# Layer 0 of a four-layer kernel: where VectorE takes the channel statistics, and which PSUM bank the gate's first product uses

## The chip, the core and the metric

The kernel runs on one core of a Trainium2 chip, in float32 throughout. The metric is the device time of one execution in microseconds (us), lower is better. TensorE is written PE (its weight loads PEld), VectorE DVE, ScalarE ACT, GpSimd POOL, and SyncE, which issues most of the DMAs, SP.

## What is computed

Four layers in a row on a batch of four 64 x 64 images with 128 channels. The change lies in layer 0, and in what layer 0 hands to layer 1. Cut to those, the reference is:

```python
# layer 0: neighbourhood attention (7 x 7 keys for each pixel, 4 heads of 32), gated
qkv = (x @ qkv_w + qkv_b).reshape(B, H, W, 3, HEADS, HEAD_DIM)
scores = einsum('bxyhd,bxyklhd->bxyhkl', q, kwin) + bias
attn_out = einsum('bxyhkl,bxyklhd->bxyhd', softmax(scores), vwin) @ proj_w + proj_b
gate = sigmoid(relu(x @ g1_w + g1_b) @ g2_w + g2_b)
x = attn_out * gate + x

# layer 1: begins with a group norm over the whole image, 32 groups of 4 channels
mean, var = mean and variance of x over (H, W, the 4 channels of a group)
h = (x - mean) * rsqrt(var + 1e-6) * scale + bias
# then full attention over the 4096 pixels, and x + o
```

The statistics of the title are the mean and the variance of each channel of layer 0's output, which layer 1's group norm needs. The gate's first product is `x @ g1_w`. Layers 2 and 3 (a gated product with a layer norm, and a selective scan in four directions) are not touched.

## The kernel before

**Stages.** The four images go through layer 0 and layer 1 one after the other. Layers 2 and the front part of 3 of an image run inside layer 1's loop and shortly after it; the scans of layer 3 and the output come at the end, for all four. Layer 0 of the next image begins (its first two chunks and its first score blocks) beside the last steps of the image before; a generator is advanced by two steps at a time there (lines 1107 and 1108).

**Layer 0's loop.** An image of 4096 pixels is 32 blocks of 8 x 16 pixels, and 8 chunks of 512 pixels; a chunk is four blocks. The loop at line 522 runs over `i`, and in one turn works on several blocks at different ages. In this order:

- `score(i + 3)`: four products q k, one for each head (32 rows of the contraction each, L456), into four PSUM banks; then four reductions on DVE (L460) that add the bias and take the maximum;
- `value(i - 1)`: the product with v (L502) into a bank `po`, which ACT copies to `oT` (L507);
- `normalise(i + 1)`: a reciprocal on DVE (L480), four scalings on POOL (L482);
- `project(i - 2)`: the product with proj (L512) into a bank `pp`, which DVE adds to x with the gate (L513);
- `by_key(i, 0)` and `by_key(i, 1)`: transposes of the probabilities (L491), copied out by ACT and by DVE (L493);
- `soften(i + 2)`, first half: two exponentials on ACT (L474);
- `take_in(n + 2, part)`, one of four parts of a chunk that is two chunks ahead: part 0 transposes x (and makes `gate_of` of the chunk before, L402), part 1 the products `pq` and `pk`, part 2 the product `pv` (L384), which DVE empties into `vt` (L386), part 3 the gate's first product `pg` (L391), which ACT empties with a Relu (L393);
- `by_key(i, 2)`, with ACT's copy, and the second half of `soften(i + 2)`;
- every fourth turn from `i` = 6 on, `hand_on(n)`: the four finished blocks of chunk n are transposed (L412), ACT copies them to `hT` (L414), and DVE takes the statistics of that copy (`bn_stats`, L415).

So in four turns of the loop there is one of each part of `take_in` and one `hand_on`. Part 2 falls in the turn just after a `hand_on`, part 3 in the turn after that. The gate's product and `pv` come up to chunk 7, that is in turns up to `i` = 20 and 19; there are eight `hand_on`, at `i` = 6, 10, ... 34.

**What sets the order.** Each engine works its instructions off in its own order. In layer 0 the instructions of PE, ACT and DVE are pinned (`pin`, L349): they stay in the order in which the program writes them. An instruction that waits holds all those behind it on its engine.

**PSUM.** There are eight banks, in three rings: "s" (four banks, `ps_s`, L149), "t" (two, `ps_t`, L152) and "o" (two, `ps_o`, L155). A new tile of a ring takes the bank of the tile that was taken one full ring earlier, and its first product waits until that tile has been emptied. The scores take four "s" banks in each turn; `pq`, `pk`, `pv` and `pg` take one each. After `pv`, the fourth score of the next turn takes the bank of `pv`; after `pg`, the fourth score of the next turn takes the bank of `pg`. In "o" lie `po`, `pp` and the gate's second product `pg2` (L400).

Of the kernel before, what the change touches and what calls it, by code (L numbers as in the profile page):

```python
# [34 lines left out]
CH = 512  # L35
NCH = L // CH
HEADS, HD, KS = 4, 32, 7
NEG = -1.0e30
GH = 64
# [99 lines left out]
def layers_0_to_2(  # L139
    ctx, tc, xf, mata, matb, rows, rpb, convw, sel, ident, cl, dram, big, ring, early, x3_d, ub_d, zf_d, y_d, dbl_d, ct_d, gw_d, bw_d  # L140
):
    nc = tc.nc
    wp = ctx.enter_context(tc.tile_pool(name="wa", bufs=1))
    tmp = ctx.enter_context(tc.tile_pool(name="tmp", bufs=2))
    sml = ctx.enter_context(tc.tile_pool(name="sml", bufs=3))
    psp = ctx.enter_context(tc.tile_pool(name="psA", bufs=1, space=PSUM))


    def ps_s(shape, name):  # L149
        return psp.tile(shape, F32, name=name, tag="s", bufs=4)  # L150

    def ps_t(shape, name):  # L152
        return psp.tile(shape, F32, name=name, tag="t", bufs=2)

    def ps_o(shape, name):  # L155
        return psp.tile(shape, F32, name=name, tag="o", bufs=2)
# [11 lines left out]
    def m(name, p=P):  # L168
        a, e = MA[name]
        return ma[0:p, a:e] if e <= nma else once[0:p, a - nma:e - nma]  # L170

    def rw(name, tiles=None):
        a, e = ROW[name]
        r = row[:, a:e] if e <= nrow else once[:, NMA - nma + a - nrow:NMA - nma + e - nrow]
        return r if tiles is None else r.unsqueeze(1).to_broadcast([P, tiles, r.shape[-1]])
# [25 lines left out]
    for cv, n in enumerate(cols_of):  # L201
        t = t_d[cv].rearrange("q h d k -> (q h) (d k)")
# [85 lines left out]
    def in_blocks(t, n=4):  # L288

        return t.rearrange("p (r b c) -> p r b c", b=n, c=BC)  # L290
# [46 lines left out]
    def layer_0(b, xt, edge_t):  # L337
# [5 lines left out]
        hT = ring([P, L], f"hT_{b}")  # L343
        st = sml.tile([P, NCH, 6], F32, name="st1", tag="st1", bufs=1)
# [4 lines left out]
        def pin(ins):  # L349
            return tc.keep_in_program_order(ins)  # L350
# [3 lines left out]
        def take_in(n, part):  # L354


            if part == 0 and n > 0:
                gate_of(n - 1)
            if n == NCH:
                return  # L360
            if part == 0:
                pt = ps_t([P, 4, P], "pt")
                for k in range(4):
                    pin(nc.tensor.transpose(pt[:, k, :], xt[:, 4 * n + k, :], ident))
                x = part_of[n] = tmp.tile([P, CH], F32, name="xT", tag="xT", bufs=4)
                pin(nc.scalar.copy(in_blocks(x), pt.rearrange("p b (r c) -> p r b c", c=BC)))
            elif part == 1:
                x = part_of[n]
                pq = ps_s([P, CH], "pq")
                pin(nc.tensor.matmul(pq, lhsT=ma[:, q0:q0 + C], rhs=x, start=True, stop=True))  # L370
                pin(nc.scalar.activation(
                    qT[:, 4 * n:4 * n + 4, :].rearrange("p b (r c) -> p r b c", c=BC), in_blocks(pq), AF.Identity,
                    bias=sbq0, scale=HD ** -0.5,
                ))
                pk = ps_s([P, CH], "pk")
                pin(nc.tensor.matmul(pk, lhsT=ma[:, k0:k0 + C], rhs=x, start=True, stop=True))
                pin(nc.scalar.activation(
                    kT[:, BR * n:BR * n + BR, :].rearrange("p r w -> p (r w)"), pk, AF.Identity, bias=cl("bk0")
                ))
            elif part == 2:  # L380
                x = part_of[n]
                pv = ps_s([P, 4, C], "pv")
                for k in range(4):
                    pin(nc.tensor.matmul(pv[:, k, :], lhsT=x[:, bass.ts(k, P)], rhs=ma[:, v0:v0 + C], start=True, stop=True))  # L384
                vt = tmp.tile([P, 4, C], F32, name="vt", tag="c512", bufs=9)
                pin(nc.vector.tensor_tensor(vt, pv, rw("bv0", 4), ALU.add))  # L386
                nc.sync.dma_start(v_d[b][CH * n:CH * n + CH, :].rearrange("(k p) c -> p k c", p=P), vt)
            else:
                x = part_of.pop(n)
                pg = ps_s([GH, CH], "pg")  # L390
                pin(nc.tensor.matmul(pg, lhsT=m("g1"), rhs=x, start=True, stop=True))  # L391
                g1 = tmp.tile([GH, 4, P], F32, name="g1", tag="g1")
                pin(nc.scalar.activation(  # L393
                    g1.rearrange("p b (r c) -> p r b c", c=BC), in_blocks(pg), AF.Relu, bias=cl("g1b", p=GH)
                ))
                part_of[n] = g1

        def gate_of(n):
            g1 = part_of.pop(n)
            pg2 = ps_o([P, 4], "pg2")  # L400
            for k in range(4):
                pin(nc.tensor.matmul(pg2[:, k:k + 1], lhsT=g1[:, k, :], rhs=cl("g2w", p=GH), start=True, stop=True))  # L402
            g = gate[:, 4 * n:4 * n + 4]
            pin(nc.scalar.activation(g, pg2, AF.Exp, bias=ng2b, scale=-1.0))
            pin(nc.vector.tensor_scalar(g, g, 1.0, None, ALU.add))
            pin(nc.vector.reciprocal(g, g))

        def hand_on(n):

            pt = ps_t([P, 4, P], "pt")  # L410
            for k in range(4):
                pin(nc.tensor.transpose(pt[:, k, :], xt[:, 4 * n + k, :], ident))  # L412
            h = hT[:, bass.ts(n, CH)]
            pin(nc.scalar.copy(h, pt.rearrange("p k t -> p (k t)")))  # L414
            pin(nc.vector.bn_stats(st[:, n, :], h))  # L415

        def bias_in(i):

# [50 lines left out]
        def soften(i, heads):  # L469
            k = blocks[i]  # L470
            if heads[0] == 0:
                k.sm = sml.tile([P, HEADS], F32, name="sm0", tag="sm0", bufs=4)
            for h in heads:
                pin(nc.scalar.activation(  # L474
                    k.pr[:, h], k.pr[:, h], AF.Exp, bias=k.mx[:, h:h + 1], accum_out=k.sm[:, h:h + 1]
                ))

        def normalise(i):
            k = blocks[i]
            pin(nc.vector.reciprocal(k.sm, k.sm))  # L480
            for h in range(HEADS):
                nc.gpsimd.tensor_scalar(k.pr[:, h], k.pr[:, h], k.sm[:, h:h + 1], 1.0, ALU.mult, ALU.mult)  # L482
            k.prT = []

        def by_key(i, g, evac):
            k = blocks[i]
            if g < len(k.tiles):
                at, n, _ = k.tiles[g]
                pt = ps_t([P, HEADS, P], "pt0")
                for h in range(HEADS):  # L490
                    pin(nc.tensor.transpose(pt[0:n, h, :], k.pr[:, h, at:at + n], ident))  # L491
                prT = tmp.tile([P, HEADS, P], F32, name="prT0", tag="c512", bufs=9)
                pin(evac(prT[0:n], pt[0:n]))  # L493
                k.prT.append(prT)

        def value(i):
            k = blocks[i]
            po = ps_o([P, P], "po0")
            for g, (at, n, slot) in enumerate(k.tiles):
                for h in range(HEADS):  # L500
                    hp = slice(HD * h, HD * h + HD)
                    pin(nc.tensor.matmul(  # L502
                        po[hp, :], lhsT=vs[0:n, slot, hp], rhs=k.prT[g][0:n, h, :],
                        start=(g == 0), stop=(g == len(k.tiles) - 1),
                    ))
            k.oT = tmp.tile([P, P], F32, name="oT0", tag="oT")
            pin(nc.scalar.copy(k.oT, po))  # L507

        def project(i):
            k = blocks.pop(i)  # L510
            pp = ps_o([P, C], "pp0")
            pin(nc.tensor.matmul(pp, lhsT=k.oT, rhs=m("proj"), start=True, stop=True))  # L512
            pin(nc.vector.scalar_tensor_tensor(xt[:, i, :], pp, gate[:, i:i + 1], xt[:, i, :], ALU.mult, ALU.add))  # L513
# [8 lines left out]
        for i in range(-3, NT + 5):  # L522
            if i + 3 < NT:
                score(i + 3)
            if 0 <= i - 1 < NT:
                value(i - 1)
            if 0 <= i + 1 < NT:
                normalise(i + 1)
            if 0 <= i - 2 < NT:
                project(i - 2)  # L530
            if 0 <= i < NT:
                by_key(i, 0, nc.scalar.copy)
                by_key(i, 1, nc.vector.tensor_copy)
            if 0 <= i + 2 < NT:
                soften(i + 2, (0, 1))
            n, part = divmod(i + 3, 4)
            if n + 2 < NCH or (n + 2, part) == (NCH, 0):
                take_in(n + 2, part)
            if 0 <= i < NT:
                by_key(i, 2, nc.scalar.copy)  # L540
            if 0 <= i + 2 < NT:
                soften(i + 2, (2, 3))
            if i >= 6 and (i - 6) % 4 == 0 and (i - 6) // 4 < NCH:
                hand_on((i - 6) // 4)
        handed[b] = hT, st


# [935 lines left out]
```

## Time and profile before

| | us |
|---|---|
| three runs, median (lowest to highest) | 3831.19 (3826.19 to 3833.25) |
| the profiled execution, its time | 3828.72 |
| its span, first to last instruction | 3826.9 |
| the four stretches of layer 0, from the first score to the last statistics | 33 to 217, 799 to 961, 1579 to 1741, 2354 to 2515 |
| busy in the second of these, 162.00 us: PE, PEld, DVE, ACT, POOL | 152.32, 104.01, 98.02, 126.65, 82.82 |

The stretches are taken from the timeline: the first score matmul of an image, and the sum-up of its statistics at layer 1's begin (L550). The first stretch holds waits for DMAs at the kernel's start as well. A profile shows one execution; its times are those of that execution, and a busy PE is not PE at its peak, since matmuls overlap. In the rows of a timeline the columns are: start, length, engine, line, operation, what is written and read, shape, number of instructions merged in the row, and in brackets how long the engine stood idle before it and what ended that. A row "x8" of L456 holds the four heads' scores, two passes for each head.

### The profile page before, as it was taken

The page shows a single profiled execution, that of the slowest core. Times are in us where ns is not written, and L with a number is a line of the kernel's source. Part 1 is how long each engine was busy: PE and PEld are TensorE (multiplying, and loading weights), DVE is VectorE, ACT ScalarE, POOL GpSimd, SP SyncE. Part 2 cuts the span into 40 slices and gives each one's busy share as a digit, 9 for nine tenths or more (in the row PEclk, how much of TensorE's full clock was granted, in tenths as well). Part 3 has the DMA queues.
Part 4 walks back from the last instruction along what each step waited for, and adds up shares of the span by engine and source line. Part 5 has one row for each costly group of instructions (what it writes and reads, how often), then busy time and mean ns, then how long its engine had stood idle before and what let it go on. Part 6 is the DMA issues. An engine that isn't in the chain of part 4 may idle for free.

```text
span 3826.9 us, 69375 instructions
## 1 busy us (share of the span) xinstructions
PE 3401.1 (89%) x26780; PEld 2787.6 (73%) x26780; DVE 2829.9 (74%) x4865; ACT 2681.4 (70%) x4350; POOL 1420.2 (37%) x1562
## 2 busy tenths in 40 slices
PE   6999999999899999998999999989999987666647
PEld 4679989966799889667998897669888863222236
DVE  3657777756677788666787886667877866999968
ACT  3865667778676776686766776866767756999934
POOL 5510012245122122352122223522221326999866
PEclk8999999999999999999999999999999996555579
DMA  5100000131010012310211112100101148999998
GB/s 141 47 3 25 12 18 29 43 99 35 18 42 32 32 62 82 121 43 1 74 66 48 51 52 94 46 1 23 41 31 59 57 166 220 232 220 204 213 276 280
DMA packets 205199, 319.30 MB, mean 83 GB/s; under 512 B 23583, under 2 KB 112188, under 8 KB 200732
## 3 DMA queue, kind: packets, MB, share of 16 engines
q1 hardware_dynamic: 165572, 237.57, 18.2%
q0 software_dynamic: 19776, 68.56, 9.8%
q10 hardware_dynamic: 19520, 8.73, 0.8%
q8 instruction: 211, 3.46, 0.4%
q14 instruction: 120, 0.98, 0.1%
HBM read 150.91 MB, written 155.56 MB: 80 GB/s over the span
## 4 chain that ended last, share of the span: by engine, by line
PE 49%; DVE 24%; ACT 9%; POOL 8%; issue 6%; DMA 2%; SPq 1%; POOLq 0%; ACTq 0%; DVEq 0%
PE po L640 15%; PE sc L607 14%; POOL inp L1210 4%; DVE mx L619 4%; DVE acc L858 3%; DVE st L633 3%; POOL y L1249 3%; PE pt L491 3%; DVE mx L614 3%; PE sc L456 2%; PE po L502 2%; ACT st L634 2%; ACT pr L474 2%; ACT st L610 2%; PE pz L808 1%
## 5 line engine op out<-in xcount | busy, mean ns | idle before, releaser
L640 PE MATMUL po<-v,st 128*128 128x129 f32 x8192 | 1081.3, 275 | 4.1 <-ACT st L634 4.1
L607 PE MATMUL sc<-qT,kT 128*128 128x128 f32 x8192 | 1081.9, 276 | 0.4 <-ACT st L610 0.4
L607 PEld LDWEIGHTS sc<-qT,kT 128*128 128x128 f32 x8192 | 1003.5, 193 | 21.9 <-issue 18.1
L640 PEld LDWEIGHTS po<-v,st 128*128 128x128 f32 x8192 | 998.8, 192 | 5.4 <-issue 5.4
L610 ACT COPY st<-sc 128x512 f32<-128x512 f32 x1024 | 577.8, 583 | 527.0 <-PE sc L607 519.6
L633 DVE TENSOR_TENSOR st<-st,pb 128x2048 f32<-128x2048 f32 x256 | 573.9, 2283 | 47.7 <-PE pb L630 47.1
L614 DVE TENSOR_TENSOR mx<-mx,st 128x1024 f32<-128x1024 f32 x256 | 315.3, 1232 | 239.3 <-ACT st L610 237.4
L634 ACT ACTIVATE st<-st 128x2048 f32<-128x2048 f32 x256 | 483.4, 1908 | 6.4 <-DVE st L633 4.7
L1199 PE MATMUL pdt<-dbl,dt 8*128 8x512 f32 x512 | 309.0, 1082 | 142.4 <-ACT de L1206 142.0
L1210 POOL TENSOR_TENSOR inp<-de,ub 128x1024 f32<-128x1024 f32 x128 | 412.1, 4479 | 36.0 <-ACT de L1206 29.0
L1199 PEld LDWEIGHTS pdt<-dbl,dt 8*128 8x128 f32 x512 | 114.4, 312 | 334.1 <-ACT de L1206 270.7
L704 POOL TENSOR_TENSOR x<-x,row 128x512 f32<-128x512 f32 x32 | 49.9, 1559 | 788.9 <-PE pt L274 788.9
L482 POOL TENSOR_SCALAR pr<-pr,sm 128x308 f32<-128x308 f32 (+3 forms) x512 | 243.5, 494 | 259.8 <-DVE sm L480 187.6
L849 POOL TENSOR_TENSOR gsum<-gsum,tp 128x504 f32<-128x504 f32 (+1 forms) x176 | 254.1, 1446 | 122.7 <-ACT gsum L837 83.9
L474 ACT ACTIVATE pr<-pr,mx 128x308 f32<-128x308 f32 (+3 forms) x512 | 262.5, 517 | 0.0
L619 DVE TENSOR_TENSOR mx<-mx 128x512 f32<-128x512 f32 (+2 forms) x384 | 256.9, 669 | 6.1
L1234 DVE TENSOR_TENSOR_SCAN h<-h,end,inp 128x1024 f32<-128x1024 f32 x96 | 221.1, 2346 | 14.7 <-POOL inp L1210 7.0
L491 PE MATMUL pt<-ident,pr 128*88 128x128 f32 (+5 forms) x1472 | 204.1, 276 | 7.8 <-ACT prT L493 7.8
L1249 POOL DMA_DIRECT2D y<-yo x112 | 206.5, 2823 | 7.3 <-DVE yo L1248 3.8
L460 DVE CUSTOM_DVE_ANT_0 pr<-sc,bias_m 128x266 f32<-128x266 f32 (+1 forms) x384 | 151.7, 451 | 69.6 <-PE sc L456 64.7
L858 DVE SCALAR_TENSOR_TENSOR acc<-xh,cc,acc 128x512 f32<-128x512 f32 (+3 forms) x244 | 196.4, 832 | 3.8 <-ACT acc L822 2.7
L491 PEld LDWEIGHTS pt<-ident,pr 128*88 128x88 f32 (+5 forms) x1472 | 163.6, 138 | 45.4 <-ACT prT L493 31.6
(233 smaller groups left out, 5254.7 us busy)
## 6 DMA issues: line engine op xcount, KB each, us to landing
y<-yo POOLq DMA_DIRECT2D x112, 512.0 KB, 10.4
y<-du SPq DMA_DIRECT2D x160, 256.0 KB
zf_d<-zf SPq DMA_DIRECT2D x64, 256.0 KB
ub_d<-u SPq DMA_DIRECT2D x64, 256.0 KB
ub<-ub_d SPq DMA_DIRECT2D x16, 1024.0 KB
yl<-y SPq DMA_DIRECT2D x64, 256.0 KB
zc<-zf_d SPq DMA_DIRECT2D x64, 256.0 KB
x<-in_x SPq DMA_DIRECT2D x128, 64.0 KB
```

Source lines behind the costliest of these rows:

```text
L474: pin(nc.scalar.activation(k.pr[:, h], k.pr[:, h], AF.Exp, bias=k.mx[:, h:h + 1], accum_out=k.sm[:, h:h + 1]))
L491: pin(nc.tensor.transpose(pt[0:n, h, :], k.pr[:, h, at:at + n], ident))
L607: nc.tensor.matmul(ps[:, r, :], lhsT=kT[:, bass.ts(G * g + r, P)], rhs=qT[:, bass.ts(i, P)], start=True, stop=True)
L610: nc.scalar.copy(k.st[:, G * g:G * g + G, :], ps)
L614: nc.vector.tensor_tensor(k.mx, k.mx, k.st[:, 4 * g - 4:4 * g + 4, :], ALU.max)
L619: nc.vector.tensor_tensor(mx[:, 0:n, :], mx[:, 0:n, :], mx[:, n:2 * n, :], ALU.max)
L633: nc.vector.tensor_tensor(part, part, pb.unsqueeze(1).to_broadcast([P, 16, P]), ALU.add)
L634: nc.scalar.activation(part, part, AF.Exp)
L640: nc.tensor.matmul(k.po, lhsT=k.st[:, j, :], rhs=v[:, j, :], start=(j == 0), stop=(j == NT - 1))
L1199: nc.tensor.matmul(pdt[j][:, g, :], lhsT=dt[o:o + RANK, P * f:P * f + P], rhs=at(dbl[o:o + RANK, :], k & 2, g0, g0 + CH), start=True, stop ...
L1210: nc.gpsimd.tensor_tensor(by_rows(inp), by_rows(de), at(ub_s[f], b ^ (k & 1), SC * n, SC * n + SC), ALU.mult)
L1249: nc.gpsimd.dma_start(here if f == 1 and k == 3 else there, yo, accum_op=ALU.add)
```

## The change

The statistics leave `hand_on` and become a function of their own. `hand_on(n)` keeps its place at `i` = 6 + 4n. `statistics(n)` is called at the end of the next turn, `i` = 7 + 4n, so that on DVE it stands behind that turn's reductions, reciprocal, `project`, copy of `by_key(i, 1)` and, where there is one, `vt`. For the last chunk it stays in the same turn as `hand_on`. And `pg` is taken from the ring "o" instead of "s".

```diff
             else:
                 x = part_of.pop(n)
-                pg = ps_s([GH, CH], "pg")
+                pg = ps_o([GH, CH], "pg")
                 pin(nc.tensor.matmul(pg, lhsT=m("g1"), rhs=x, start=True, stop=True))
...
-            h = hT[:, bass.ts(n, CH)]
-            pin(nc.scalar.copy(h, pt.rearrange("p k t -> p (k t)")))
-            pin(nc.vector.bn_stats(st[:, n, :], h))
+            pin(nc.scalar.copy(hT[:, bass.ts(n, CH)], pt.rearrange("p k t -> p (k t)")))
+
+        def statistics(n):
+            pin(nc.vector.bn_stats(st[:, n, :], hT[:, bass.ts(n, CH)]))
...
-            if i >= 6 and (i - 6) % 4 == 0 and (i - 6) // 4 < NCH:
-                hand_on((i - 6) // 4)
+
+            n, part = divmod(i - 6, 4)
+            if 0 <= n < NCH and part == 0:
+                hand_on(n)
+            if 0 <= n < NCH and part == (1 if n < NCH - 1 else 0):
+                statistics(n)
```

No instruction is added or taken away, and the same numbers are computed from the same data.

## The prediction

> **What bounds the kernel now.** I read the page first (which engine is full), then the row of the moved instruction, then the busy times of one period of layer 0, and last the order of time on VectorE and TensorE inside that period.
>
> ```profile
> span 3826.9 us, 69375 instructions
> PE 3401.1 (89%) x26780; PEld 2787.6 (73%) x26780; DVE 2829.9 (74%) x4865; ACT 2681.4 (70%) x4350; POOL 1420.2 (37%) x1562
> ...
> L415 DVE BATCH_NORM_STATS2 st<-hT x32: 693/695/697, 101.7 to 2513.6; 128x6 f32<-128x512 f32 x32
> its engine sat idle before it (us, times) until:
>   ACT hT L414: 86.1, 32
> ...
> 890.29:911.06 20.77, 19.96 (x215) 14.01 (x215) 12.50 (x53) 16.64 (x51) 10.89 (x25) 1.00 0.15 44
> ```
>
> The first two lines are the page: TensorE is the full engine. The next are the row of the statistics: VectorE stands idle 86.1 us before 32 of them (2.7 us each) until ScalarE has copied hT. The last is one period of layer 0 (four blocks of queries): columns are length, then busy time of PE, PEld, DVE, ACT, POOL, then the clock. VectorE is busy 12.50 of 20.77 us, so its 86.1 us of idleness are not themselves the price. TensorE is busy 19.96, and I ask where it is held.
>
> ```profile
> 907.02 0.69 DVE L415 BATCH_NORM_STATS2 st<-hT 128x6 f32<-128x512 f32 x1 [3.68 <-ACT hT L414]
> 907.63 0.46 DVE L460 CUSTOM_DVE_ANT_0 pr<-sc,bias_m 128x308 f32<-128x308 f32 x1
> ...
> 909.73 0.68 DVE L493 COPY prT<-pt 95x512 f32<-95x512 f32 x1
> 910.33 0.68 DVE L386 TENSOR_TENSOR vt<-pv,row 128x512 f32<-128x512 f32 x1
> ...
> 899.71 0.80 PE L456 MATMUL sc<-kT,qT 32*128 32x308 f32 x8
> 900.44 0.86 PE L502 MATMUL po<-prT,v 110*32 110x128 f32 x24
> ...
> 906.97 1.04 PE L491 MATMUL pt<-ident,pr 128*95 128x128 f32 x8
> 908.15 1.16 PE L384 MATMUL pv<-ma,xT 128*128 128x128 f32 x8
> 909.15 0.60 PE L491 MATMUL pt<-ident,pr 128*76 128x128 f32 x4
> 909.68 0.72 PE L456 MATMUL sc<-kT,qT 32*128 32x266 f32 x6
> 911.06 0.71 PE L456 MATMUL sc<-kT,qT 32*128 32x266 f32 x2 [0.66 <-DVE vt L386]
> 911.70 0.54 PE L502 MATMUL po<-prT,v 95*32 95x128 f32 x12
> ```
>
> These are timelines of VectorE, then of TensorE. The statistics start at 907.02, so the score reductions (L460), the copy L493 and vt (L386) behind them are late. The fourth head's score matmul takes the bank that vt empties: three heads go at 909.68, the fourth at 911.06. The four heads of block 21 (899.71) took 0.73 us together, and a head by itself takes 0.64 (911.06 to 911.70). So a late fourth head delays TensorE by almost its whole lateness, of which the page's idle figure, 0.66, shows half.
>
> The second edit has its own trace of the same kind:
>
> ```profile
> 894.59 1.10 PE L456 MATMUL sc<-kT,qT 32*128 32x266 f32 x8
> 895.62 0.86 PE L502 MATMUL po<-prT,v 95*32 95x128 f32 x24
> ...
>   ACT g L393: 6.1, 16
> ...
> 825.51 1.04 PE L491 MATMUL pt<-ident,pr 128*114 128x128 f32 x8
> 826.38 1.06 PE L384 MATMUL pv<-ma,xT 128*128 128x128 f32 x8
> ...
> 827.47 0.69 DVE L386 TENSOR_TENSOR vt<-pv,row 128x512 f32<-128x512 f32 x1 [0.21 <-PE pv L384]
> ```
>
> One block after the gate product pg, the four heads take 1.03 us (894.59 to 895.62) where 0.64 would do: ScalarE's Relu on pg (894.25 to 894.92 on its timeline) holds the fourth head's bank. The third line, from the row of the score matmuls, counts waits on that Relu. The last three show a period start without statistics in front: there vt waits only for pv.
>
> **What the Trainium skill says.** "PSUM — Partial Sum Buffer", section "Engine vs sequencer instructions", says that the queues of ScalarE, VectorE and GpSimd are strict FIFO; the 3.68 us wait with ready scores behind it agrees. "TensorE: Matmul & The Clock Gate", section "The mechanism", has products on different row groups overlap; the trace agrees, eight passes of four heads in 0.73 us against 0.64 for one head's two. "Perfetto Trace Analysis", section "Optimization Strategy", reads a gap that repeats on the engine that should be full as a possible lack of buffers; the 0.66 us gap, once every 20.77 us, is one, released by the emptying of a bank.
>
> **The change part by part.** No instruction is added or removed, and no DMA is issued or moved past: SP's and POOL's queues keep their orders.
>
> *Statistics (28 of 32; the last of each batch stays).* They now stand behind vt in the next block. Without the wait, that block's reductions start when the first score is there: 905.12 + 0.82 (as 899.71 to 900.53 in the period before) = 905.94 instead of 907.63, 1.69 earlier. The copy L493 could then start at 909.73 − 1.69 = 908.04; its transposes allow 906.97 + 1.07 (825.51 to 826.58 at the earlier start) = 908.04 too. TensorE's pv needs the first reduction, now long done, so it follows its transposes by 0.87 as at 825.51 to 826.38: 907.84 instead of 908.15. From pv, vt starts 1.09 later (826.38 to 827.47): 908.93. The fourth head comes 0.73 after vt (910.33 to 911.06): 909.66. The other three start at 909.68 − 0.31 = 909.37, so a lateness of 0.29 stays. The next product starts at 909.66 + 0.64 = 910.30 instead of 911.70: **1.40 us per period**. Each of the four batches has such periods at blocks 11, 15, 19 and 23: 16 × 1.40 = 22.4 us. The statistics themselves, 0.61 us of VectorE, now run from 909.53 to 910.14, and the next scores arrive at 909.37 + 0.75 = 910.12: covered. Without this cover they would cost up to 0.6 × 28 = 17 us.
>
> Three later hand-ons of each batch have no pv. There the lateness reaches TensorE through the reductions and the copy L493. After the one at 926.08 the score group lasts 1.08 us (927.97 to 929.05), 0.44 too long; after the one at 941.65 the value product is spread over 1.21 us instead of 0.86, 0.35. The third has no scores behind it. Sum 0.8 × 4 = 3.2 us; in that stretch TensorE also waits 0.24 us per block for ScalarE's copies, which may take part of it, so between 0 and 3.2, and I take 2.4.
>
> *pg in an "o" bank.* The fourth head no longer waits for the Relu: 1.03 − 0.64 = 0.39 us at blocks 8, 12, 16, 20 and 24, 5 × 4 × 0.39 = 7.8 us. At a batch's start two more heads wait on it (blocks 0 and 4, fourth head 0.84 and 0.90 late). Block 0 is followed by a product that needs the Relu, and behind block 4 ScalarE has only 0.27 us of idleness; I take 0.5 each, for the three batches that do not start under DMA waits: 3.0, between 0 and 5.2.
> The price: the two "o" banks also serve po and pp. pg must wait until oT has been copied out of po: that copy ends at 912.96 (912.69 + 0.27), pg runs at 913.79, 0.83 us of slack. Behind pg in the ring comes pp at 917.18, long after the Relu's end (915.02 + 0.67). Cost 0, and if the cover is gone, the lateness of oT above 0.83 us, with all of TensorE queued behind pg.
>
> **The sum.** 22.4 + 2.4 + 7.8 + 3.0 = 35.6 us. The period becomes 20.77 − 1.40 − 0.39 = 18.98 us; ScalarE, the next engine, needs 16.64 of it. In the block before the statistics ScalarE is without a gap (902.20 to 907.15 on its timeline), but it was waiting for TensorE at both ends of it (0.51 before, 0.46 after), so it does not end the wait. The profiled execution took 3828.72 us (span 3826.9 and 1.8 around it): 3793.1. The median of the three runs is 2.5 us above it: 3831.19 − 35.6 = 3795.6, I say 3796.
>
> **Rivals.**
> *Half of it.* vt or a ScalarE copy stays late and ends the wait in place of the statistics. For it: the fourth head still depends on vt, and at block 7, where no statistics stand, it is late by 0.85 us. Against: block 7 has no third group of transposes between pv and the scores, which at 909.15 fills 0.53. If only the 0.66 of visible idleness and 0.2 for pv come back, 16 × 0.86 + 7.8 = 21.6, less what ScalarE keeps: gain 14 to 24, about 3812.
> *Nothing.* VectorE's idleness was covered and each regained gap reappears at the next wait. For it: VectorE has 8 us idle per period. Against: TensorE's own wait names vt and the Relu. 3831.
> *Slower.* The ring of "o" is too short: two banks for po, pp, pg and pg2. Where ScalarE copies oT later than 0.83 us after now, pg blocks TensorE's queue, 24 times in the loops (six a batch). It outweighs the 35.6 us from 35.6 / 24 = 1.5 us of stall each, so oT 2.3 us late; at 2 us each: 48 − 35.6 = 12 us slower, 3843. For it: ScalarE is 80% busy. Against: its idle time just before oT is 1.19 us at 912.69.
>
> **How the numbers follow.** The forecast 0.66, half 0.19, nothing 0.06, slower 0.09. About 0.2%, 7.7 us, is what a measurement of this kernel can tell from no change. The forecast's bounds: all unknowns low, 16 × 1.40 + 7.8 = 30.2; all high, with the residual 0.29 gone too, 35.1 for these two and 3.2 and 5.2 = 43.5. That is 3788 to 3801; to leave out no more than two in ten the range must take in most of "half", so it ends at 3816. Faster by more than 0.2%: 0.66 + 0.19 = 0.85; within: 0.06; slower: 0.09.
>
> **What would show it.** Right: the 86.1 us at the statistics gone (except the four last ones); the fourth head of blocks 11, 15, 19 and 23 within 0.3 us of the other three, with pv following its transposes at once; no score matmul waiting for the Relu; a period of about 19 us, the gain in the four layer-0 stretches alone and layers 1 to 3 as they were. Wrong: a period above 20 us, a wait of pg, po or pp on ScalarE's oT or Relu, VectorE busy when the scores of blocks 11, 15, 19 and 23 arrive, or a lower granted clock (1.00 now) in the period.

## The result, and the profile after

| | before | after |
|---|---|---|
| median of four runs, us (lowest to highest) | 3831.84 (3826.19 to 3833.25) | 3790.33 (3786.84 to 3794.29) |
| the profiled execution, us | 3828.72 | 3789.72 |
| its span, us | 3826.9 | 3787.9 |
| layer-0 stretches, first score to the sum-up of the statistics, us | 184.4, 161.1, 159.4, 159.4 | 177.0, 149.4, 149.4, 149.4 |

The kernel became faster by 41.5 us: ratio 0.9895, 95% interval 0.9878 to 0.9912, that is 34 to 47 us. The forecast was 3796, 35.6 us less than before. The two profiled spans differ by 39.0 us, and the four layer-0 stretches by 7.4 + 11.6 + 10.0 + 10.0 = 39.0. Everything else together (the start, layers 1 to 3, the scans and the output) took the same time to 0.1 us, made up of single differences of +3.3, -1.2, -0.2, -1.6 and -0.3. That these cancel is luck: over the ten traces of this document that keep both banks of "o", the same code takes 3155 to 3163 us. Nor can the 7.4 us of the first stretch be relied on, since that stretch lies under DMA waits and takes 173 to 190 us in those ten. Of the second stretch's 11.6 us, 1.7 are a low clock in the trace of before (last section). A stretch without these two disturbances is 10.0 us shorter, and this the traces show twice.

Of the kernel before, what ended the idle time ahead of the score matmuls (longest only), and blocks 20 to 24 of the second batch (length; PE, PEld, DVE, ACT, POOL; clock, DMA share, GB/s):

```profile
its engine sat idle before it (us, times) until:
  DVE vt L386: 33.1, 44
...
894.59:915.35 20.76, 19.96 (x215) 14.01 (x214) 12.49 (x52) 16.62 (x51) 10.88 (x24) 1.00 0.15 43
```

From the profile after: the row of the statistics, the row of the score matmuls (what TensorE waited for before them), and the busy times of blocks 20 to 24 of the second batch.

```profile
L417 DVE BATCH_NORM_STATS2 st<-hT x32: 679/682/694, 104.7 to 2476.2; 128x6 f32<-128x512 f32 x32
its engine sat idle before it (us, times) until:
  ACT hT L414: 3.5, 4
...
L458 PE MATMUL sc<-kT,qT x1024: 335/439/877, 32.7 to 2460.8; 32*128 32x266 f32 x64, 32*128 32x308 f32 x64, 32*128 32x209 f32 x22, 32*128 32x242 f32 x21
its engine sat idle before it (us, times) until:
  issue: 22.9, 97
  DVE prT L495: 6.1, 19
  DVE vt L387: 5.3, 12
...
881.85:900.87 19.02, 19.02 (x216) 13.68 (x215) 12.46 (x52) 16.53 (x51) 10.84 (x25) 1.00 0.16 47
```

VectorE's 86.1 us of waiting for hT are down to 3.5, the four last chunks that kept their place. TensorE's waits for vt before the scores (weight loads and matmuls counted together, so most waits twice) fell from 33.1 us in 44 cases to 5.3 in 12, and the Relu (6.1 us before) is gone from the list. A period of four blocks takes 19.02 us instead of 20.76, at the same clock of 1.00. The same place of the period, first VectorE's timeline, then TensorE's:

```profile
894.96 0.68 DVE L495 COPY prT<-pt 95x512 f32<-95x512 f32 x1
895.83 0.69 DVE L387 TENSOR_TENSOR vt<-pv,row 128x512 f32<-128x512 f32 x1 [0.20 <-PE pv L385]
896.44 0.68 DVE L417 BATCH_NORM_STATS2 st<-hT 128x6 f32<-128x512 f32 x1
897.04 0.42 DVE L462 CUSTOM_DVE_ANT_0 pr<-sc,bias_m 128x266 f32<-128x266 f32 x1
...
893.86 1.04 PE L493 MATMUL pt<-ident,pr 128*95 128x128 f32 x8
894.74 1.06 PE L385 MATMUL pv<-ma,xT 128*128 128x128 f32 x8
895.63 0.60 PE L493 MATMUL pt<-ident,pr 128*76 128x128 f32 x4
896.16 1.13 PE L458 MATMUL sc<-kT,qT 32*128 32x266 f32 x8
897.22 0.86 PE L504 MATMUL po<-prT,v 95*32 95x128 f32 x24
```

The order is as planned: copy, vt, statistics, next reductions. vt no longer comes late; it waits 0.20 us for TensorE. From the transposes (893.86) to the value product (897.22) TensorE needs 3.36 us; before it was 4.73 (906.97 to 911.70). The score group still lasts 1.06 us where a free one of this width takes 0.66 (experiment 2): the fourth head goes late, and yet no idle time stands in brackets, and TensorE counts as busy 19.02 of 19.02 us.

### The profile page after: what moved, and what is told of

It is laid out like the page before. It is cut to its first block, busy times and chain, and to the rows that moved or that the text cites. A ratio compares the mean times of both kernels' runs of the same rounds, so it can differ in the third digit from the quotient of the medians.

```text
span 3787.9 us, 69412 instructions
## 1 busy us (share of the span) xinstructions
PE 3375.8 (89%) x26780; PEld 2780.8 (73%) x26780; DVE 2838.1 (75%) x4865; ACT 2679.2 (71%) x4350; POOL 1421.5 (38%) x1562
## 4 chain that ended last, share of the span: by engine, by line
PE 54%; DVE 22%; POOL 8%; ACT 7%; issue 6%; DMA 3%; SPq 1%; POOLq 0%; DVEq 0%; ACTq 0%
PE po L646 15%; PE sc L613 15%; DVE mx L625 4%; POOL inp L1216 4%; PE pt L493 4%; DVE acc L864 4%; DVE st L639 3%; DVE mx L620 3%; POOL y L1255 2%; PE po L504 2%; PE sc L458 2%; ACT st L640 2%; ACT st L616 2%; PE pp L514 1%; PE pz L814 1%
## 5 line engine op out<-in xcount | busy, mean ns | idle before, releaser
L484 POOL TENSOR_SCALAR pr<-pr,sm 128x308 f32<-128x308 f32 (+3 forms) x512 | 244.2, 498 | 220.4 <-DVE sm L482 190.3
```

## The experiments

All runs are compared by the layer-0 stretches of the second to the fourth batch, and by the period of blocks 20 to 24 of the second batch. The first stretch is left out for its DMA waits. While both banks of "o" are there, the other three agree to 0.1 us within an execution, but for 1.6 to 1.7 us that a batch of some executions loses at its start under a lower clock (shown in the last section). The other stages, whose code is the same in all of them, vary by up to 4 us each from trace to trace. Times and ratios are medians of four executions where an interval is given, else of one execution.

**1. Each part alone.** First the statistics only (pg stays in "s"):

```diff
-                pg = ps_o([GH, CH], "pg")
+                pg = ps_s([GH, CH], "pg")
```

> Only the statistics are moved; pg stays in an s bank. Theory (two separate waits, each on the bank of one take-in product, that add up): the period falls by 1.38 us (16 of them), a tail of 0.77 per batch, so about 27 us less than before, 3805; the Relu's 0.37 us at blocks 8 to 24 stays. Rival (the two edits need each other: with the first wait gone the Relu's takes its place): period above 20.3 us, gain under 12 us, 3820 or more.

Measured: 3803.23 us, ratio to before 0.9924 (0.9910 to 0.9939), stretches of 152.7, period 19.38. Then pg only (the statistics are called in the turn of `hand_on`):

```diff
-            if 0 <= n < NCH and part == (1 if n < NCH - 1 else 0):
+            if 0 <= n < NCH and part == 0:
                 statistics(n)
```

> Only pg is moved to an o bank; the statistics stay in hand_on. Theory: 0.37 us at five blocks of each batch and 1.4 us at the start of each of the last three, 11 to 12 us less than before, 3820; the fourth head of blocks 11, 15, 19 and 23 stays 1.4 us behind the others. Rival (the Relu's wait is covered by the statistics' wait in the same period): under 4 us gained, 3828 or more.

Measured: 3817.63 us, ratio 0.9961 (0.9946 to 0.9976), stretches of 156.1, 157.7 (1.6 of it lost at its start under a low clock) and 156.1, period 20.40. The busy times of the two periods, the statistics moved alone and then pg moved alone:

```profile
886.20:905.58 19.38, 19.38 (x215) 13.96 (x214) 12.50 (x52) 16.63 (x51) 10.80 (x25) 1.00 0.16 46
```

```profile
894.67:915.07 20.40, 19.59 (x215) 13.72 (x214) 12.48 (x52) 16.52 (x51) 10.88 (x24) 1.00 0.15 44
```

20.76 falls by 1.38 and by 0.36, and by 1.74 with both: the two waits are separate and add up. By the medians of the timed runs, 29.3 and 14.9 us against 41.5 for both; the sum of 44.2 differs from 41.5 by less than the runs of one kernel scatter (7.5 us).

**2. What still holds TensorE.** The changed kernel with `pv` in the ring "o" too, so that no score waits for vt:

```diff
-                pv = ps_s([P, 4, C], "pv")
+                pv = ps_o([P, 4, C], "pv")
```

> The changed kernel with pv in an o bank as well. Theory (what still holds TensorE is the fourth head's wait for vt, 0.40 us at blocks 11, 15, 19, 23 and 0.83 us at blocks 3 and 7): that wait is gone, 16 x 0.40 + 7 x 0.83 = 12 us less than the changed kernel, about 3779; all heads of a block together. Rival (two o banks are too few for po, pp, pg, pg2 and pv, so that pv waits for oT or pp for vt): no faster than the changed kernel, 3790 or more.

Measured: 3778.55 us, ratio to before 0.9858 (0.9843 to 0.9872), stretches of 146.95. TensorE's timeline of this kernel at the same place:

```profile
892.98 1.06 PE L385 MATMUL pv<-ma,xT 128*128 128x128 f32 x8
893.87 0.60 PE L493 MATMUL pt<-ident,pr 128*76 128x128 f32 x4
894.40 0.73 PE L458 MATMUL sc<-kT,qT 32*128 32x266 f32 x8
895.06 0.86 PE L504 MATMUL po<-prT,v 95*32 95x128 f32 x24
...
880.09:898.71 18.62, 18.62 (x215) 13.38 (x214) 12.43 (x52) 16.40 (x51) 10.82 (x24) 1.00 0.17 48
```

The score group takes 0.66 us (894.40 to 895.06) and the period, in the last line, 18.62: the 0.40 us were there to be had though TensorE was 100% busy by the profile. In the trace the gain is 0.40 at each of blocks 11, 15, 19 and 23 and 0.84 at block 7. Block 3's 0.83 was swallowed by the transposes right behind its scores: in the second batch they take 1.83 us up to pg instead of 1.02. So a stretch gains 2.44, not 3.26. The expectation for the whole, 3779, was met by the median of the runs, 11.8 us under the changed kernel; by the traces that was partly luck, since the three comparable stretches support 7.3 us and a first stretch like them would bring it to 9.8. Whether `pv` in "o" would do as well with the statistics left in `hand_on` was not run.

With `pq` and `pk` there as well:

```diff
-                pq = ps_s([P, CH], "pq")
+                pq = ps_o([P, CH], "pq")
...
-                pk = ps_s([P, CH], "pk")
+                pk = ps_o([P, CH], "pk")
```

> As pv_in_o, with pq and pk in o banks too, so that the scores have the four s banks alone. Theory: blocks 2 and 6 lose their waits for kT (0.83 and 0.39 us), 3 to 4 us less than pv_in_o, about 3775. Rival (the ring of two fills): pq waits for oT, pv for qT, and each batch's first two chunks, whose products come with no work between, wait for their own copies; as slow as the changed kernel or slower.

Measured: 3777.79 us, ratio to before 0.9858 (0.9842 to 0.9875), stretches of 146.07, period 18.62. A stretch gains 0.88 us more, where 1.22 was expected. Blocks 2 and 6 gain 0.83 and 0.39 as foreseen and block 1 another 0.50, but block 3 loses 0.84 again: the wait that the trace names there, ahead of the transposes, is one for POOL's scaling of the probabilities (L484, 0.21 us). The timed runs can't tell this kernel from `pv` alone. These two are the fastest versions, 54 to 55 us under the kernel before by the medians of their own rounds.

**3. Is the statistics' own time covered?** The changed kernel with every statistics instruction twice, the second result unused:

```diff
             pin(nc.vector.bn_stats(st[:, n, :], hT[:, bass.ts(n, CH)]))
+            again = sml.tile([P, 6], F32, name="again", tag="again", bufs=1)
+            pin(nc.vector.bn_stats(again, hT[:, bass.ts(n, CH)]))
```

> The changed kernel with every statistics instruction issued twice, the second result unused: 0.6 us more of VectorE per chunk, behind vt. Theory (TensorE is held only by the bank of vt, and what stands behind vt on VectorE is covered up to the copy L495, which waits 0.36 us for TensorE anyway): the period grows by at most 0.2 us, a layer-0 stretch from 149.4 to at most 150.5. Rival (the cover was used up by the first one, which ends as the next scores arrive): 0.6 us per chunk, a stretch of 153 to 154.

Measured: 3791.52 us, period 19.02 as without it, the last two stretches 149.9, that is 0.5 more, all of it at the end, where the last chunk's statistics stand alone. (The second batch's 151.5 holds 1.6 us lost at its start, under the low clock of the last section.) VectorE's timeline:

```profile
896.91 0.68 DVE L417 BATCH_NORM_STATS2 st<-hT 128x6 f32<-128x512 f32 x1
897.51 0.68 DVE L419 BATCH_NORM_STATS2 again<-hT 128x6 f32<-128x512 f32 x1
898.11 0.42 DVE L464 CUSTOM_DVE_ANT_0 pr<-sc,bias_m 128x266 f32<-128x266 f32 x1
...
900.04 0.68 DVE L497 COPY prT<-pt 95x512 f32<-95x512 f32 x1
```

The second one makes the four reductions 0.6 us late. The copy behind them, which waited 0.36 us for TensorE in the changed kernel, now waits for nothing and starts 0.15 us later against its transposes, and TensorE doesn't notice.

**4. Does the place in the block matter?** The statistics in the later block, but ahead of the copy and of vt:

```diff
+            n, part = divmod(i - 6, 4)
+            if 0 <= n < NCH - 1 and part == 1:
+                statistics(n)
             if 0 <= i < NT:
                 by_key(i, 0, nc.scalar.copy)
...
-            if 0 <= n < NCH and part == (1 if n < NCH - 1 else 0):
+            if n == NCH - 1 and part == 0:
                 statistics(n)
```

> The changed kernel with the statistics in the same later block, but ahead of the copy of by_key(i, 1) and of vt. Theory (only what stands in front of vt counts): the copy then vt start 0.6 us later less the 0.2 to 0.3 that vt now waits for pv, so 0.34 us per period: a layer-0 stretch of 149.4 + 4 x 0.34 = 150.8. Rival (being behind ScalarE's copy of hT was all that mattered, the place in the later block does not): 149.4 as it is.

Measured: stretches of 150.6 to 150.7, period 19.33, so 0.31 us per period (3789.72 us in one execution; the whole time is too coarse for it). VectorE's timeline:

```profile
895.23 0.32 DVE L515 SCALAR_TENSOR_TENSOR x<-pp,gate,x 128x128 f32<-128x128 f32 x1
895.47 0.68 DVE L417 BATCH_NORM_STATS2 st<-hT 128x6 f32<-128x512 f32 x1
896.07 0.67 DVE L495 COPY prT<-pt 95x512 f32<-95x512 f32 x1
896.66 0.68 DVE L387 TENSOR_TENSOR vt<-pv,row 128x512 f32<-128x512 f32 x1
```

The same 0.6 us of VectorE costs 0.31 ahead of vt and nothing behind it. Together with experiment 2, where the waiting goes with the bank, this shows that it is the emptying of the bank of pv that TensorE waits for, not VectorE at large. Experiment 4 delays the copy and vt together and does not part them.

**5. The price of the "o" ring.** First ScalarE's copy `oT` was moved behind the copy of `by_key(i, 0)` and half of the exponentials, with pg in "o" and with pg in "s":

```diff
-            k.oT = tmp.tile([P, P], F32, name="oT0", tag="oT")
-            pin(nc.scalar.copy(k.oT, po))
+            k.po = po
+
+        def take_out(i):
+            k = blocks[i]
+            k.oT = tmp.tile([P, P], F32, name="oT0", tag="oT")
+            pin(nc.scalar.copy(k.oT, k.po))
...
                 soften(i + 2, (0, 1))
+            if 0 <= i - 1 < NT:
+                take_out(i - 1)
```

> The changed kernel with ScalarE's copy oT moved behind the copy of by_key(i, 0) and the first half of soften, about 2 us later in each block; pg lies in an o bank. Theory (the o ring is the price that the prediction named: pg waits for oT): pg is held about 1.5 us, six times a batch, and pg2 too; a stretch at least 6 us longer than that of the same delay with pg in an s bank. Rival (po and pp carry the delay in any case, pg adds nothing): the two stretches differ by no more than pg's own gain of 3.3 us, the o kernel the shorter one.

> The same delay of oT with pg in an s bank, the statistics still moved. Theory: only pg2 waits for oT, once a period, 1 to 1.5 us; a stretch of 152.7 + 6 to 10. Rival as in oT_late: about as long as oT_late or longer.

Measured: 3792.30 us and stretches of 150.5 with pg in "o"; 3809.41 us and stretches of 154.4 to 156.0 with pg in "s". Neither theory came true. The delay costs 1.1 us a stretch with pg in "o" and 1.7 with pg in "s" (154.4 against 152.7), not 6 to 10, and the "o" kernel is the shorter one by 3.8, near the 3.3 of the rival (the other two pairs hold 1.6 us of low clock besides). The pair did not make the test: pg did not wait for oT at all. ScalarE's and TensorE's timelines of the first:

```profile
899.42 0.25 ACT L513 COPY oT<-po 128x128 f32<-128x128 f32 x1
...
896.10 0.86 PE L504 MATMUL po<-prT,v 95*32 95x128 f32 x24
896.89 0.49 PE L518 MATMUL pp<-ma,oT 128*128 128x128 f32 x2
...
898.19 1.07 PE L392 MATMUL pg<-xT,ma 128*64 128x512 f32 x2
```

pg runs at 898.19, before oT is copied out of po at 899.42, so it lies in the bank of pp. With the copy of oT later in the program, pp's bank is freed first, and it seems that it is also handed out first. So the sentence above, that a new tile takes the bank of the tile taken one full ring earlier, does not hold here; this one trace fits a rule that it holds only where banks are freed in the order in which they are taken.

A second pair therefore cut the ring itself to one bank, with pg outside it and inside it (in both the eighth bank lies unused):

```diff
-        return psp.tile(shape, F32, name=name, tag="o", bufs=2)
+        return psp.tile(shape, F32, name=name, tag="o", bufs=1)
```

> The statistics moved, pg in an s bank, and the ring o cut from two banks to one (the other stays unused). This is the control of the next run: pp must wait until po has been copied out, po until pp has been added, so each block of layer 0 is longer, by 0.5 to 1 us: a stretch of 152.7 + 16 to 32. Layer 1's value product has one bank too and gets slower; only the layer-0 stretches are compared.

> The changed kernel with the ring o cut to one bank: pg shares it with po, pp and pg2. Theory (pg comes late enough in its turn, behind eight transposes, and its Relu ends before the next po): pg costs at most 0.3 us a turn even here, and its own gain stays, so the stretch is 1.5 to 3.3 us shorter than that of one_o_pg_s. Rival of the prediction (a ring too short makes pg hold TensorE, 1.5 us or more, six times a batch): the stretch is 6 us or more longer than that of one_o_pg_s.

Measured: stretches of 173.1 to 173.6 with pg outside and 169.2 to 170.1 inside. TensorE's timeline of the second, and one line of the first:

```profile
905.91 0.87 PE L504 MATMUL po<-prT,v 95*32 95x128 f32 x24
907.21 0.49 PE L514 MATMUL pp<-ma,oT 128*128 128x128 f32 x2 [0.44 <-ACT oT L509]
907.54 1.04 PE L493 MATMUL pt<-ident,pr 128*95 128x128 f32 x8
908.50 1.07 PE L392 MATMUL pg<-xT,ma 128*64 128x512 f32 x2
...
912.16 0.49 PE L514 MATMUL pp<-ma,oT 128*128 128x128 f32 x2 [0.56 <-ACT oT L509]
...
920.25 0.49 PE L514 MATMUL pp<-ma,oT 128*128 128x128 f32 x2 [0.44 <-ACT oT L509]
```

With one bank every pp waits for oT (0.44 us here), and a stretch is about 20 us longer. But pg starts 0.96 us after its transposes (907.54 to 908.50), as it does with pg in "s" and with two banks: within that time VectorE has emptied pp. The ring has a small price: one block after pg, pp waits 0.56 us for oT with pg in "o" (912.16) and 0.44 with pg in "s" (920.25), so that each pg of blocks 8 to 24 is worth 0.25 us instead of 0.37. With 0.55 and 0.64 at blocks 0 and 4 that makes 2.4 us a stretch in favour of "o", as expected. The 3.0 to 4.4 us between the stretches hold two disturbances besides: 1.6 to 1.7 us of low clock at the start of each "s" stretch, and at the end between 0.5 us in favour of "o" and 1.0 in favour of "s".

## Why the prediction was right, step by step

| step | predicted, us | in the traces, us |
|---|---|---|
| statistics, periods with pv | 16 x 1.40 = 22.4 | 16 x 1.38 = 22.1 |
| statistics, hand-ons without pv | 2.4 | 4 x (0.77 + 0.42) = 4.8 |
| pg, blocks 8 to 24 | 20 x 0.39 = 7.8 | 20 x 0.37 = 7.4 |
| pg, the starts of three batches | 3 x 1.0 = 3.0 | 3 x (0.55 + 0.88) = 4.3 |
| sum | 35.6 | 38.6 |

The right column is how much earlier each block's scores come, measured from block to block against the kernel before (behind the last block, the sum-up). It is read from the undisturbed batches and put down for all four; 38.6 stands against 39.0 for the whole span. The difference is made up of the first batch, which gained 7.4 instead of 8.6 under its DMA waits, and of block 2 of the second batch, 1.7 us slower in the profiled execution of before for its clock there (last section).

- *The periods.* pv follows its transposes by 0.88 us (0.87 predicted), vt comes 1.09 after pv (1.09), the value product 0.66 + 0.40 after the other heads (0.64 + 0.29). The residual lateness is 0.40, outside the 0.3 that was named as a sign of being right, because the other three heads came 0.1 us earlier than worked out, not because vt is later. Experiments 2 and 4 show the bank of pv to be the cause, and experiment 1 that this part stands by itself. Of the 1.38, 0.97 come at blocks 11, 15, 19 and 23, where the fourth head waits for vt; 0.41 come one block earlier, 0.30 of it because pv no longer waits for the first reduction (1.18 us behind its transposes before, 0.88 after).
- *The hand-ons without pv* were taken as 0.44 and 0.35, and then cut to 2.4 in all for what ScalarE's copies might take back. They took nothing back. The first is worth 0.77, because the value product behind the late score group was slow as well (1.05 us from its start to the next product before, 0.80 after), and so were the transposes behind that (1.38 and 1.27).
- *The starts* gave 1.43 instead of 1.0; for block 4 the prediction let ScalarE's 0.27 us of idleness take half of it, and it took nothing: 0.88 of 0.90.
- *The cover of the statistics.* Here a step was wrong. Reckoned as in the prediction, the scores arrive at 896.16 + 0.75 = 896.91, and the statistics hold VectorE until 897.04. So VectorE was busy when the scores came, which stood among the signs of being wrong, and it cost nothing. The up to 17 us that the prediction put on a missing cover do not come about either. Experiment 3 takes that cover away and the period stays at 19.02: behind the reductions there is a second cover, the copy's wait for its transposes.
- *The price of the "o" ring* was put at 0, and it is 0: in the regular part of the second batch (820 to 945) TensorE shows no wait of pg, po or pp on oT or the Relu. At a batch's start pg2 waits 0.21 us for the Relu, as foreseen for block 0.
- *The rivals.* "Half of it" and "nothing" fail on the table above. "Slower" fails by experiment 5 in the form that could be tried: even one bank is enough for pg. A ring in which pg really waits for a late oT was not made.
- *The total.* 35.6 was 3.0 us short: 3.7 by the hand-ons and the starts, less 0.7 that the periods and pg fell short. The other 2.9 us to the measured 41.5 are for the most part the choice of execution: the profiled one of before was 3.1 us under its median, the one of after 0.6 under its own. What lay behind that was not looked into. In the bounds, the sum of 35.1 should read 16 x 1.69 + 7.8 = 34.8; the end of the range at 3788 stays.

## What to carry to other kernels

An idle engine in front of one instruction is priced by what is queued behind that instruction and which buffer of the bounding engine it frees, not by the length of the wait: 2.7 us of VectorE were worth 1.4 where a bank hung on them, and 0.6 us more of VectorE behind that bank cost nothing. Where several row groups share TensorE, read the length of the group and not only the idle time: a late member costs nearly its whole lateness while the engine counts as busy. Put short-lived products that another engine empties late into a ring in which the next tenant comes late too, and look at the order in which banks are freed before saying which product gets which bank.

## What the runs showed of the hardware that was not expected

- TensorE can be busy 19.02 of 19.02 us by the profile with 0.40 us of removable waiting in it (18.62 with `pv` elsewhere); the idle times in its timeline show none of it.
- With both banks of "o", layer 0's periods of four blocks from 8 to 24 repeat to 0.02 us within an execution and where two programs share their wait (19.02 twice, 18.62 twice), while layer 1 with layers 2 and 3 in it took 582 to 585, 616 to 619 and 614 to 617 us in ten executions of ten programs that leave those stages' code alone. With one bank, 3 of 32 periods were 0.2 to 0.3 us longer than the rest.
- Early in a batch TensorE's granted clock can fall to half for some 3.4 us: at 8 of the 36 starts of the second to fourth batches in the twelve traces. The busy times of the stretch with the second batch's products of q and k, of the kernel before and then of the kernel after (columns as above, the clock is the third from the end):

```profile
803.60:807.20 3.60, 3.56 (x4) 1.17 (x4) 1.05 (x7) 1.05 (x3) 2.21 (x6) 0.53 0.20 55
```

```profile
798.60:800.60 2.00, 1.91 (x7) 0.70 (x7) 1.10 (x7) 1.11 (x3) 2.00 (x6) 1.00 0.10 28
```

  From pq to the next scores it is 3.57 us at the low clock (803.64 to 807.21) and 1.88 at the full one (798.69 to 800.57); the second window takes in three score products at its end. The Trainium skill ("TensorE: Matmul & The Clock Gate", section "Part 1: The HAM clock gate") tells of half the clock in windows of some 3.4 us that run freely, so that what falls into one varies from run to run. The trace of before agrees: from 803.64 to 807.04 the mean clock is 0.50. This is why the second batch of before reads 161.1 and not 159.4, and the 1.7 us are in the 39.0 of the two spans but not in the 38.6 of the table. Whether the change makes such windows rarer is open: they fell on 6 of 12 starts with pg in "s" and on 2 of 24 with pg in "o", and what brings them on was not tested.
